# A transformer block on one core: token numbers and gate passes in front of the first transposes, inner sums behind accumulator sums, weight sums loaded in front of x

## The chip, the cores and the metric

The kernel runs on one core of a Trainium2 chip. The core has engines with instruction queues of their own: TensorE (PE; its weight loads are shown apart, as PEld), VectorE (DVE), ScalarE (ACT), GpSimd (POOL) and SyncE (SP), and 16 DMA engines that all queues share. Each engine works its queue in order. The metric is the device time of one execution in microseconds.

## The reference

`x` holds 32 sequences of 128 tokens with 512 features. Each sequence has a condition row `t` of 512 numbers, and a mask over its tokens, which is true for the last few (the padding) only.

```
emb = silu(t) @ ada_w + ada_b                  # shift, scale, gate: 3 x 512
norm = where(mask, layernorm(x)*(1+scale) + shift, 0)
ssm  = gelu(norm @ ssm_w1 + ssm_b1) @ ssm_w2 + ssm_b2
     + gelu(norm @ bwd_w1 + bwd_b1) @ bwd_w2 + bwd_b2
x    = x + gate * where(mask, ssm, 0)
ff   = silu(t) @ ffada_w + ffada_b             # shift, scale, gate again
n    = layernorm(x)*(1+scale_ff) + shift_ff
out  = x + gate_ff * (gelu_tanh(n @ ff_w1 + ff_b1) @ ff_w2 + ff_b2)
```

All is float32. The weights ssm and bwd are 512 x 512 each, ff_w1 is 512 x 1024 and ff_w2 is 1024 x 512. The two flips in the reference cancel, since the inner functions work on single tokens.

## The kernel before

**First block, masked tokens only.** The masked tokens are numbered through all sequences into "slots". There are 512 slots in four tiles of 128 (a run-time loop at the end takes what is over). `find_slots(h)` finds for half h (256 slots) the token number of each slot: two small matmuls of `pick` against `rank` into a PSUM bank, then a comparison, a sum and an addition on VectorE (lines 221 to 238). `gather_slots` fetches these tokens' rows of x with two indirect DMAs that POOL issues (line 241). `modulation_matmuls` (line 260) multiplies silu(t) with columns of ada_w: parts 0 and 1 (shift, scale) as `pm_ss`, part 2 (gate) as `pm_g` in four passes, one for each 128 of the 512 features. `slot_part` (line 288) spreads modulation rows over slots with a matmul. A tile is normalised and modulated (`modulated`, line 166), transposed on TensorE and copied by ACT (`transposed_slots`, line 175), goes through `hidden` (line 182, matmul L188, Gelu on ACT) and `project` (line 196, L203), and `finish_slots` (line 296, L209, L210 and L298) adds gate and x and stores the result to `x1_rows` in DRAM. Weights w1, w2, fw1, ada_f, fw2 and x are loaded by SP in the order of the code. The tile `ada_f` takes the place of `ada_a`, so its load waits for the last gate pass.

**Second block, all tokens.** It works on four pairs p of 8 sequences (1024 tokens). A pair has two sides of four sequences. `take_first_half` (line 670) overwrites the masked rows of the loaded x by rows of `x1_rows`, with one indirect DMA of POOL for each sequence. Both products use Strassen-Winograd's seven products of 2 x 2 blocks, the first one twice: its seven outer products are called streams (1, 2, 5, 6, 3, 7, 4, in that order), and each is made of seven inner products P1 to P7. `TokenBlocks.one(j)` (line 768, L775) makes the outer sums of the tokens' blocks. `token_sums(j, n)` (line 825) makes the inner sums, in four parts n: L835 for j = 1 (used by stream 5), L839 for 2 (stream 6), L842 for 3 (stream 7) and L845 for 4 (stream 3). The sums of the weights are made once, in the opening, and kept in DRAM as `t_rows`; `load_weights(j)` (line 847, L852) loads one of them into a tile that it shares with the gates of the second product.

Each stream has two PSUM banks, e and a. `phase` (line 897, matmul L906) does one inner product and what follows it: P5's bank is copied by ACT (L920); `seed` copies or adds a to e after P1 (L952 on ACT, L950 on VectorE); P6's result is added to a kept sum into e (L931); P7 and P4 give sums on VectorE (L936, L941). `with_p5` (L957) and `after` (L986, L990) are sums on POOL that L931 reads. The Gelu is ACT's (L868). `window` (line 995) runs two streams against each other: in position n = 0 to 6 new P5, new P1, old P3, old P7, new P2, new P6, old P4, and after each position whatever `put(w, n, ...)` filled in. Window w has new stream STREAMS[w] and old stream STREAMS[w-1]. Streams 1 and 2 of the first pair are written out by hand (lines 1206 to 1232). Those of the next pair are started during the second product (`SecondProduct`, line 1014, matmul L1093), whose steps are filled in the same way (lines 1311 to 1358); there SP also stores the output (L1073) and loads the x of the pair after next (L328).

All five engines take their instructions in the order of the code, which nothing rearranges. PSUM tiles come from pools of two or three banks for each tag (`ps_t` "tr", `ps_h` "h", `ps_o` "o"), and a new tile waits for the one that held its bank before.

Of the kernel before, what the change touches and what calls it, by code (L numbers as in the profile page):

```python
# [9 lines left out]
F32 = mybir.dt.float32  # L10
# [12 lines left out]
def kernel(  # L23
# [51 lines left out]
    P = 128  # L75
# [144 lines left out]

    def tokens_of(picked, slots, n, name, pool):

        pl = ps_t.tile([P, 512], F32, tag="tr", name=f"pl_{name}")
        for c in range(n):
# [24 lines left out]

    def find_slots(h):  # L250
        part = slice(h * NC // 2, (h + 1) * NC // 2)
        return tokens_of(pick[:, ts(h, NH)], slot_col[:, part], NC // 2, f"s{h}", ssm)

    def gather_slots(token_i):
        both = xp.tile([P, 2, D], F32, tag="x", name=f"xc_{len(xc)}")
        for c in range(NC // 2):
            gather(both[:, c], token_i[:, c : c + 1])
            xc.append(both[:, c])
# [16 lines left out]
    def modulation(pm, mod, ada, modb, lo, hi):  # L275

        modulation_matmuls(pm, ada, lo, hi, range(KC))
        modulation_rows(pm, mod, modb, lo, hi)
# [9 lines left out]
    def slot_part(at, j, pool, tag):  # L288
        return of_slots(pick, at, mod1, j, pool, tag, f"part{j}_s{at}")
# [201 lines left out]
    pm = ps_o.tile([P, 512], F32, tag="o", name="pm_ss")  # L491
    modulation(pm, mod1, ada_a, modb_a, 0, 2)
    rows = [(slot_part(c, 1, ps_o, "o"), slot_part(c, 0, ps_h, "h")) for c in range(2)]
    pm = ps_o.tile([P, 512], F32, tag="o", name="pm_g")
    xT_s = ssm.tile([P, KC, NH], F32, tag="xT", name="xT_s0", bufs=2)
    xT_t = ssm.tile([P, KC, NH], F32, tag="xT", name="xT_s1", bufs=2)
    xn = group_of_tiles("s")
    mv, rstd = statistics(xc, "s01")
    xn_s = [
# [4 lines left out]
    ]  # L504
    modulation_matmuls(pm, ada_a, 2, 3, range(2))
    fw1 = fwp.tile([P, KC, FF], F32, name="fw1")
# [13 lines left out]
    transposed_slots(xn_s[0], xT_s[:, :, ts(0, P)], "s0")  # L520
    modulation_matmuls(pm, ada_a, 2, 3, range(2, 3))
    token_i = find_slots(1)
    gather_slots(token_i)
    transposed_slots(xn_s[1], xT_s[:, :, ts(1, P)], "s1")
    modulation_matmuls(pm, ada_a, 2, 3, range(3, KC))
    ptr = ps_t.tile([P, 512], F32, tag="tr", name="ptr_b")
# [122 lines left out]
    sp = straight.enter_context(tc.tile_pool(name="sp", bufs=1, side="right"))  # L649
    gs = [keep_gate(c, slot_part(c, 2, ps_o, "o")) for c in (2, 3)]  # L650
    modT = const.tile([P, KC, 3 * B], F32, name="modT")
# [560 lines left out]
    now.do(2, "P1")  # L1212
    now.do(1, "P2", "P5", "P6")
    of_x[0].one(4)
# [9 lines left out]
    now.with_p5(2, "12")  # L1224
    now.token_sums(1, 2)
    now.token_sums(1, 3)
    now.do(2, "P2", "P6")
    for n in range(2):
        now.token_sums(2, n)
# [3 lines left out]
    for p in range(NP):  # L1233
# [7 lines left out]
        if p:  # L1241
            for n, at in enumerate(((1, 3), (1, 4), (1, 6))):
                put(*at, now.token_sums, 2, 1 + n)
        for n, at in enumerate(((1, 6), (2, 1), (2, 1), (2, 3)) if p else ((2, 1), (2, 1), (2, 3), (2, 3))):
            put(*at, now.token_sums, 3, n)
        for n, at in enumerate(((2, 4), (2, 4), (2, 6), (2, 6))):
            put(*at, now.token_sums, 4, n)
# [71 lines left out]
        if more_pairs:  # L1319
# [29 lines left out]
            if p + 2 < NP:  # L1349
                x_of[p + 2] = [[], []]  # L1350
                put(11, lambda: x_of[p + 2][0].extend(load_side(p + 2, 0)))
                put(13, lambda: x_of[p + 2][1].extend(load_side(p + 2, 1)))
            put(12, lambda: nxt["p"].do(1, "P2", "P6"))
            put(13, lambda: nxt["p"].load_weights(2))
        for step in range(2, len(ORDER)):
            second.step(step)
            for f in fill.get(step, ()):
                f()
# [120 lines left out]
```

## Time and profile before

| | us |
|---|---|
| Median of 3 runs | 465.48 (463.76 to 468.08) |
| The profiled execution's own time | 462.27 |
| Its span, first to last instruction | 460.6 |
| First L188 matmul (hidden layer of the slots) | 21.31 |
| First L906 matmul (streams of the first pair) | 87.81 |
| First L1093 matmul (second product of the first pair) | 131.52 |
| VectorE's L1067 in the last step of the first pair | 186.57 |

In a row of the timeline stand the start and the length in microseconds, the engine (with q: its queue, which issues a DMA), the line, the operation, the tile written and the tiles read, the shape, the number of instructions merged, and in brackets the engine's idle time before it with what ended it. In the rows of slices each digit stands for 11.5 us and gives the busy share in tenths. Weight loads run beside matmuls, so a wait is often shown at PEld.

### The profile page before, as it was taken

How to read it: one execution, taken by the hardware profiler on the slowest of the kernel's cores; microseconds unless marked ns; L12 is line 12 of the kernel's file. 1: busy time of each engine (PE TensorE's matmuls, PEld its weight loads, DVE VectorE, ACT ScalarE, POOL GpSimd, SP SyncE). 2: the span in 40 equal slices, each digit the busy share in tenths (PEclk: the TensorE clock that was granted, in tenths of full speed). 3: DMA queues.
4: the chain of work that ended last, by engine and by line, in shares of the span. 5: the costliest groups of instructions: out<-in, count | busy, mean ns of one | idle time of the engine just before them, and what ended most of it. 6: DMA issues, size and time to landing. Idle time of an engine off the chain costs nothing.

```text
span 460.6 us, 5827 instructions
## 1 busy us (share of the span) xinstructions
PE 447.5 (97%) x2000; PEld 364.8 (79%) x2000; DVE 331.0 (72%) x538; ACT 175.4 (38%) x380; POOL 157.5 (34%) x153
## 2 busy tenths in 40 slices
PE   6899999989999999999999999999999999999995
PEld 2385385677888888888888888888888888888884
DVE  4649768999779739986787498867973995434645
ACT  3122021744355371344454614444446154552000
POOL 6210083038981000489700005887000026560000
PEclk9999999999999999999999999999999999999999
DMA  8999835693306743823077248220872342222022
GB/s 273 386 406 360 322 130 85 204 310 94 141 5 216 103 94 110 324 93 139 1 228 112 73 162 311 91 97 3 236 107 70 133 165 80 81 88 97 0 84 102
DMA packets 82419, 70.42 MB, mean 153 GB/s; under 512 B 63168, under 2 KB 63696, under 8 KB 81362
## 3 DMA queue, kind: packets, MB, share of 16 engines
q1 hardware_dynamic: 67298, 57.03, 39.6%
q0 software_dynamic: 4480, 11.66, 7.0%
q10 hardware_dynamic: 10608, 1.32, 2.0%
q8 instruction: 17, 0.28, 0.2%
q14 instruction: 16, 0.13, 0.1%
HBM read 56.83 MB, written 13.17 MB: 152 GB/s over the span
## 4 chain that ended last, share of the span: by engine, by line
PE 74%; DVE 10%; SPq 4%; DMA 3%; issue 3%; ACT 3%; POOL 2%; ACTq 0%; DVEq 0%; POOLq 0%
PE a_o L1093 17%; PE a_m L906 16%; PE e_o L1093 13%; PE e_m L906 12%; PE ph_s L188 6%; PE po_s L203 4%; SPq L745 4%; DMA tw<-t_rows 2%; ACT xT L728 1%; DVE sx L835 1%; DVE xT L726 1%; DVE s L775 1%; PE part_s L283 1%; PE pm_f L263 1%; PE last L1093 1%
## 5 line engine op out<-in xcount | busy, mean ns | idle before, releaser
L957 POOL TENSOR_TENSOR ha<-p_m,ha 128x512 f32<-128x512 f32 x20 | 26.0, 1298 | 151.3 <-ACT ha L964 142.0
L1093 PE MATMUL e_o<-fw,ha 128*128 128x256 f32 x256 | 57.9, 379 | 0.0
L728 ACT ACTIVATE xT<-xT,modT 128x128 f32<-128x128 f32 x112 | 44.1, 480 | 30.8 <-DMA xT<-xn 30.8
L1093 PE MATMUL a_o<-t,hb 128*128 128x256 f32 x240 | 54.1, 379 | 0.0
L1093 PEld LDWEIGHTS e_o<-fw,ha 128*128 128x128 f32 x256 | 48.7, 190 | 6.6
L1093 PEld LDWEIGHTS a_o<-t,hb 128*128 128x128 f32 x240 | 45.6, 190 | 6.2
L674 POOL DMA_INDIRECT x<-x_rows,slot_i x32 | 36.0, 1126 | 29.3 <-DMA x_rows<-t_s 18.0
L868 ACT ACTIVATE hb<-hb,biasT 128x256 f32<-128x256 f32 x64 | 29.0, 500 | 29.1 <-POOL hb L990 19.4
L957 POOL TENSOR_TENSOR hb<-p_m,hb 128x512 f32<-128x512 f32 x20 | 29.1, 1454 | 19.2 <-DVE hb L936 18.9
L920 ACT COPY p_m<-e_m 128x512 f32<-128x512 f32 x27 | 15.8, 585 | 49.1 <-PE e_m L906 49.1
L964 ACT COPY ha<-e_m 128x512 f32<-128x512 f32 x32 | 18.5, 578 | 27.5 <-PE e_m L906 25.9
L1093 PE MATMUL e_o<-fw,s 128*128 128x256 f32 x128 | 28.9, 379 | 0.0
L1093 PE MATMUL a_o<-fw,ha 128*128 128x256 f32 x128 | 28.9, 379 | 0.0
L1093 PE MATMUL a_o<-t,s 128*128 128x256 f32 x128 | 28.9, 379 | 0.0
L188 PE MATMUL ph_s<-xT_s,w 128*128 128x256 f32 x128 | 28.6, 382 | 0.0
L203 PE MATMUL po_s<-w,h_s 128*128 128x512 f32 x64 | 28.6, 592 | 0.0
L188 PEld LDWEIGHTS ph_s<-xT_s,w 128*128 128x128 f32 x128 | 24.0, 190 | 4.6 <-ACT h_s L192 1.5
L1093 PEld LDWEIGHTS e_o<-fw,s 128*128 128x128 f32 x128 | 24.3, 190 | 3.3
L1093 PEld LDWEIGHTS a_o<-t,s 128*128 128x128 f32 x128 | 24.3, 190 | 3.3
L1093 PEld LDWEIGHTS a_o<-fw,ha 128*128 128x128 f32 x128 | 24.3, 190 | 3.3
L868 ACT ACTIVATE ha<-e_m,biasT 128x256 f32<-128x256 f32 x48 | 20.0, 468 | 15.4 <-PE e_m L906 14.0
L931 DVE TENSOR_TENSOR e_m<-a_m,ha 128x512 f32<-128x512 f32 x20 | 13.9, 697 | 16.4 <-POOL ha L957 6.6
(210 smaller groups left out, 869.2 us busy)
## 6 DMA issues: line engine op xcount, KB each, us to landing
tw<-t_rows SPq DMA_DIRECT2D x16, 896.0 KB, 5.1
x<-in_x_dram SPq DMA_DIRECT2D x16, 512.0 KB, 6.6
gate<-gate_rows POOLq DMA_DIRECT2D x8, 1024.0 KB, 5.1
out_dram<-x SPq DMA_DIRECT2D x15, 512.0 KB, 3.0
xT<-xn SPq DMA_DIRECT2D x92, 64.0 KB, 2.5
fw<-in_L_cond_ff_w_dram SPq DMA_DIRECT2D x2, 2048.0 KB, 10.6
ada_f<-in_L_cond_ffada_w_dram SPq DMA_DIRECT2D x4, 768.0 KB, 15.9
ada_a<-in_L_cond_ada_w_dram SPq DMA_DIRECT2D x4, 512.0 KB, 5.4
```

The lines of the kernel that those rows point to most:

```text
L188: nc.tensor.matmul(ph[:, :n], w[:, k, ts(f, P)], xT[:, k, :], start=(k == 0), stop=(k == KC - 1))
L203: nc.tensor.matmul(po, h[f][:, ts(i, P)], w[:, f, :], start=(f == 0), stop=(f == HC - 1))
L674: nc.gpsimd.indirect_dma_start(out=xs[i // G][i % G // 2][:, i % 2], out_offset=None, in_=x1_rows[:slots, :], in_offset=bass.IndirectOffse ...
L728: nc.scalar.activation(out, src, AF.Identity, bias=shift, scale=scale)
L745: queues[b % len(queues)].dma_start(dst[ts(q, R), b], src[ts(b, R), q])
L868: nc.scalar.activation(dst[:, n], src[:, n], AF.Gelu_apprx_tanh, bias=biasT[:, f : f + 1])
L906: nc.tensor.matmul(bank[:, ts(n, QT)], self.w_block(j, product)[:, ts(n, P)], self.x_block(j, product), start=(product in ("P1", "P5") and ...
L920: nc.scalar.copy(p5, e)
L931: nc.vector.tensor_tensor(e, a, p5, add)
L957: nc.gpsimd.tensor_tensor(self.place(RESULT[j], c), self.p5[j], other, ALU.add)
L964: nc.scalar.copy(self.place(RESULT[j], c), src)
L1093: nc.tensor.matmul(part, src[:, k, ts(i, P)], w[product][:, k, :], start=(last and k == 0), stop=True, skip_group_check=True,)
```

## The change

It has five parts.

1. `tokens_of` and `find_slots` take the PSUM bank as an argument. The second half's `find_slots` and `gather_slots` move up, directly behind `pm_ss`, and use a bank of `ps_h`. All four gate passes of `pm_g` are done in one place, in front of the first transposes; before, two were there, one stood behind each of the two transposes.
2. The gate of slot tile 3 is spread into a bank of `ps_h` in place of `ps_o`.
3. In the hand-written start of the first pair, stream 1's P5 comes before its P2, and `token_sums(1, 2)` and `(1, 3)` come behind stream 2's P2 and P6, so that on VectorE L931 stands in front of them.
4. In the windows, `token_sums(3, n)` and `(4, n)` move to later positions in the first pair; in the later pairs one part, `token_sums(3, 2)`, moves from (2, 1) to (2, 3), behind the L936 there.
5. In steps 11 to 13 of the second product, `load_weights(2)` of the next pair is issued in front of the load of side 1 of the x of the pair after next.

```diff
-    def tokens_of(picked, slots, n, name, pool):
+    def tokens_of(picked, slots, n, name, pool, bank=(ps_t, "tr")):
-        pl = ps_t.tile([P, 512], F32, tag="tr", name=f"pl_{name}")
+        pl = bank[0].tile([P, 512], F32, tag=bank[1], name=f"pl_{name}")
...
-    def find_slots(h):
+    def find_slots(h, *bank):
...
     modulation(pm, mod1, ada_a, modb_a, 0, 2)
+    gather_slots(find_slots(1, (ps_h, "h")))
...
-    mv, rstd = statistics(xc, "s01")
+    mv, rstd = statistics(xc[:2], "s01")
...
-    modulation_matmuls(pm, ada_a, 2, 3, range(2))
+    modulation_matmuls(pm, ada_a, 2, 3, range(KC))
...
     transposed_slots(xn_s[0], xT_s[:, :, ts(0, P)], "s0")
-    modulation_matmuls(pm, ada_a, 2, 3, range(2, 3))
-    token_i = find_slots(1)
-    gather_slots(token_i)
     transposed_slots(xn_s[1], xT_s[:, :, ts(1, P)], "s1")
-    modulation_matmuls(pm, ada_a, 2, 3, range(3, KC))
...
-    gs = [keep_gate(c, slot_part(c, 2, ps_o, "o")) for c in (2, 3)]
+    gs = [
+        keep_gate(2, slot_part(2, 2, ps_o, "o")),
+        keep_gate(3, slot_part(3, 2, ps_h, "h")),
+    ]
...
     now.do(2, "P1")
-    now.do(1, "P2", "P5", "P6")
+    now.do(1, "P5", "P2", "P6")
...
     now.with_p5(2, "12")
-    now.token_sums(1, 2)
-    now.token_sums(1, 3)
     now.do(2, "P2", "P6")
+    for n in range(2, 4):
+        now.token_sums(1, n)
...
-        for n, at in enumerate(((1, 6), (2, 1), (2, 1), (2, 3)) if p else ((2, 1), (2, 1), (2, 3), (2, 3))):
+        for n, at in enumerate(((1, 6), (2, 1), (2, 3), (2, 3)) if p else ((2, 3), (2, 3), (2, 4), (2, 4))):
             put(*at, now.token_sums, 3, n)
-        for n, at in enumerate(((2, 4), (2, 4), (2, 6), (2, 6))):
+        for n, at in enumerate(((2, 4), (2, 4), (2, 6), (2, 6)) if p else ((2, 6), (2, 6), (3, 1), (3, 1))):
             put(*at, now.token_sums, 4, n)
...
                 put(11, lambda: x_of[p + 2][0].extend(load_side(p + 2, 0)))
-                put(13, lambda: x_of[p + 2][1].extend(load_side(p + 2, 1)))
             put(12, lambda: nxt["p"].do(1, "P2", "P6"))
             put(13, lambda: nxt["p"].load_weights(2))
+            if p + 2 < NP:
+                put(13, lambda: x_of[p + 2][1].extend(load_side(p + 2, 1)))
```

## The prediction

> **What bounds the kernel now.** I read the page's busy times first, then its slices, then the timeline of each stretch in which TensorE pauses, then the waits and the landing times of the transfers.
>
> ```profile
> PE 447.5 (97%) x2000; PEld 364.8 (79%) x2000; DVE 331.0 (72%) x538; ACT 175.4 (38%) x380; POOL 157.5 (34%) x153
> DVE  4649768999779739986787498867973995434645
> DMA  8999835693306743823077248220872342222022
> ```
>
> TensorE is busy for 447.5 of 460.6 us, so no reordering can win more than 13 us, and most of that lies in the first 6 us and in the starts of short matmuls. The digits (11.5 us each) show two other things: the DMA engines are full in the first five slices (0 to 55 us), and VectorE is full in slice 8 (92 to 104 us). The pauses of TensorE lie in these places, with what stands in front of them:
>
> ```profile
> 33.04 1.23 DVE L317 TENSOR_TENSOR t<-fw 128x1024 f32<-128x1024 f32 x1 [2.15 <-DMA fw<-in_L_cond_ff_w_dram]
> ...
> 52.11 0.42 DVE L639 TENSOR_SCALAR modb_f<-modb_f 32x512 f32<-32x512 f32 x1
> ...
> 52.60 0.69 DVE L209 TENSOR_TENSOR t_s<-po_s,b 128x512 f32<-128x512 f32 x1
> ...
> 60.62 1.77 POOL L674 DMA_INDIRECT x<-x_rows,slot_i  x1 [0.31 <-issue]
> ...
> 64.17 0.69 DVE L706 BATCH_NORM_STATS2 st<-x 128x6 f32<-128x512 f32 x1 [1.05 <-DMA x<-x_rows,slot_i]
> ...
> 89.80 0.73 PEld L906 LDWEIGHTS e_m<-xT,fw 128*128 128x128 f32 x4 [0.50 <-ACT e_m L952]
> ...
> 96.36 1.74 POOL L957 TENSOR_TENSOR hb<-p_m,hb 128x512 f32<-128x512 f32 x1 [18.91 <-DVE hb L936]
> 96.89 3.44 DVE L835 TENSOR_TENSOR sx<-xT 128x512 f32<-128x512 f32 x2
> 98.07 1.71 POOL L957 TENSOR_TENSOR ha<-p_m,ha 128x512 f32<-128x512 f32 x1
> 100.58 0.68 DVE L931 TENSOR_TENSOR e_m<-a_m,ha 128x512 f32<-128x512 f32 x1
> 101.32 0.73 PEld L906 LDWEIGHTS e_m<-s,fw 128*128 128x128 f32 x4 [1.65 <-DVE e_m L931]
> ...
> 103.23 1.17 POOL L674 DMA_INDIRECT x<-x_rows,slot_i  x1 [3.45 <-DMA x<-in_x_dram]
> ...
> 120.02 0.70 DVE L931 TENSOR_TENSOR e_m<-a_m,ha 128x512 f32<-128x512 f32 x1 [2.03 <-POOL ha L986]
> ```
>
> From 33.04 (ff_w1 landed) VectorE runs without a break of more than 0.15 us to 52.53, and L209, the first step towards the second x1 store, starts 0.08 after that. At 101.32 TensorE has waited for L931, which sat on VectorE behind the inner sums of L835.
>
> ```profile
> 189.86 1.59 SPq L328 DMA_DIRECT2D x<-in_x_dram  x2
> 191.50 0.46 SPq L852 DMA_DIRECT2D tw<-t_rows  x1
> 198.68 1.10 PE L906 MATMUL e_m<-xn_sy,tw 128*128 128x256 f32 x4 [0.52 <-DMA tw<-t_rows]
> ```
>
> The weight sums of stream 6 are issued behind two x loads, land at 198.55, and TensorE has waited for them.
>
> I count a pause as the time between two matmul starts above their usual 0.216 us, and add about 0.1 for the slower first matmul after it: 0.36 at 89.80, 0.25 at 93.51, 0.26 at 94.63, 1.51 at 101.32, 0.48 at 105.26, 0.40 at 110.14, 0.27 each at 120.78 and 122.78, 0.76 at 198.68, 0.3 at 289.62.
>
> **The change, part by part.**
>
> *Opening.* Two gate passes move from behind the first transposes to in front of them (1.04 us each, at 17.90 and 20.10), the token numbers of the second half (matmuls 0.71; VectorE 0.42 + 0.42 + 0.16; two POOL gathers 1.06 + 0.98) from 18.9 to about 11.5. On TensorE the token matmuls fall into the 0.79 wait for the modulation rows. The four gate passes run 14.2 to 18.1, where it had waited 1.25 for xn_s. Second transposes then end at about 19.5 instead of 20.18, the ACT copy (0.58) follows, and L188 starts at 20.3 to 20.9 instead of 21.31: I take 0.8 early. On VectorE the 1.0 us fits before the first gather lands (13.73). On POOL the gathers stand before rstd (15.75): ready at 13.3, they end at about 15.7, so rstd slips by 0.1 to 0.5; its cover is TensorE's gate passes. ada_f, which waits on SP for the last gate pass, is issued 3 us earlier, into a full queue.
>
> TensorE's 0.8 is not the end's. The chain from 33.04 to the second x1 store is VectorE's, and only the 0.08 before L209 is TensorE's. Of the rest, modT and the weight sums (L657, L581) come 0.7 earlier and so may leave the third gather alone, which took 1.77 beside them against 1.00 for its neighbours: 0 to 0.7 saved on the way to 64.17 and so to the transposes at 79.06, where TensorE waits for xn (L718, ends 79.40). The second gathers' 512 KB now pass in front of w1 and w2: at 387 GB/s (1 MB took 2.71 us) 1.36 us later, against ssm_w1's landing at 17.16 and use at 20.3, bwd_w1's at 19.87 and use after 26. Behind w2 they no longer delay ff_w1, but it lands after the same bytes; I bound that at 0.5 either way. Sum: -0.35, between -0.9 and +0.5.
>
> The first gathers landed 4.7 us after their issue, beside ada_w, and moved 333 GB/s of one 1.5 us stretch against 63 for SP's queue. The Trainium skill (DMA: Bandwidth & Descriptors, Queues, rings and completion order) says that each DMA engine takes turns between queues packet by packet. By this rule the gathers take about half of the engines, and w1 is 1.36 us late at most, by the row all of that at once; neither brings ssm_w1 past 18.5, so the sum is the same by both.
>
> *P5 before P2 (line 1213).* The copy L952 stands behind 16 scalings on ACT until 89.17; now P5 (0.86) runs beside it. P6 still starts after the second block sum (90.76), L931 waits for P6 instead of p_m and starts at 92.35, not 92.75: -0.4 for everything on VectorE up to L1182. The 0.36 is gained once; 93.51 and 94.63 move with it.
>
> *Inner sums behind accumulator sums (0 to 131 us).* L931 of stream 2 is put ahead of two L835, but it also reads ha, which POOL's second L957 writes. Shifted by 0.4, that ends between 97.67 + 1.27 (POOL's time alone at 111.34) and 97.67 + 1.71 (beside VectorE): 98.94 to 99.38; I take the upper, since one L835 still runs beside it. L931 ends at 99.7 to 100.1, the two L835 add 1.0, and L839 starts at 100.6 to 101.1 against 101.19: VectorE wins 0.1 to 0.55. (What now waits behind L931, two L835 and then L839, is first read by TensorE in stream 5's P3, at 108.0, and stream 6's P5, at 106.2.) From there to the sum of stream 5's P7 (L936, 110.81) it has the same instructions and is full; the pauses at 101.32, 105.26 and 110.14 change places rather than add up. TensorE's own slack there (111.51 against 111.97) lets it gain 0.6 to 1.0 by 112. Next late is POOL: six gathers and six sums without a break from 103.23 to L931 at 120.02, released by the x load, whose issue stands behind L1182. Issued 0.4 earlier into DMA engines that were 73% busy at 96 to 98, it lands 0 to 0.45 earlier. So -0.3, between -0.85 and 0; the 120.78 pause stays. Rows of later pairs (one L842 behind L936) show no pause: 0.
>
> The two L835 took 1.75 beside POOL and 0.68 alone. The Trainium skill (SBUF — State Buffer, Who interferes with whom) says that a VectorE instruction with two SBUF inputs and a reading GpSimd instruction exclude each other, the later one waiting whole. This agrees, and speaks against the change: the time in which L835 was locked out is now spent waiting for L957. By the rule the second L957 ends at 99.38 and VectorE wins 0.1; by the row of POOL alone 0.55. POOL's chain allows the same either way.
>
> *Weight sums in front of x (line 1351).* SP waits at 189.86 for an output store; tw's tile is free when L1067 ends (187.26), so it can go after the store's issue at 188.40, 3.1 us earlier. It took 5.9 to 7.0 us with x beside it: lands 194.3 to 195.5, needed at 198.0. -0.76, and -0.3 at 289.62; nothing in the last two pairs, which load no x. Behind it on SP stand only these x loads, and the next issue is at 204.99; x lands up to 2.3 later (896 KB): 195.5 for the tile of the gather at 198.48.
>
> *Banks.* pl_s1 and one gate tile move to the other pool, whose third-last tile is free by 35.5: 0.
>
> **Sum:** -0.35 - 0.3 - 0.76 - 0.3 = -1.7. The profiled execution took 462.27 (span 460.6): 460.6 after. The median shown, 465.48, is 3.2 above it; shifted alike, 463.8.
>
> **Rivals.**
> - *All pauses pay in full.* 0.8 + 3.26 (89 to 110) + 1.06 = 5.1: 460.4. For it: TensorE is 97% busy, and each pause stands on it. Against: VectorE full at 98 to 112, L718 at 79.4.
> - *It does nothing that lasts:* POOL and DMA keep their times and the tw landing is replaced by another wait: 465.3. For it: the full DMA queue and POOL's chain.
> - *Slower: x behind tw.* POOL's gathers are in order, with L957 behind them. If tw takes 7.04 from 188.4 and x 4.9 after it (191.45 to 196.32), x lands at 200.4, 2 us late for 198.48. POOL's slack to L931 (204.65, less the 0.76) is 1.7 after a landing at 197.6, so it decides from 199.3 on; 1.1 lost in each of two pairs, less the 1.7 of the sum: +0.5, 466.0, and a microsecond more for each half microsecond that x lands later still. Against: the three transfers together ended at 198.55.
>
> **Chances:** forecast 0.62, all pauses 0.10, nothing 0.17, slower 0.11. About 1% (4.7 us) is what a measurement of this kernel tells from no change. Only the first rival with a little spread passes it on one side (0.08), and a heavier version of the last on the other (0.05). The forecast's own range is 462.4 to 465.3; with the rivals, and medians of three that came from 463.76 to 468.08, 461.0 to 466.4.
>
> **What would show it.** L188 starts near 20.5, yet L209 of the second store stays near 52.5; L931 near 99.5 behind POOL; TensorE's pause at 120.8 remains; none before 6's P5 near 197. Wrong if ff_w1 lands more than 1 us off 33.04, if POOL's gathers start late in pairs 1 and 2, or if TensorE keeps the 0.8 at 79.

## The result, and the profile after

The changed kernel takes 465.05 us (median, 462.11 to 466.86) against 465.2 (462.04 to 469.57) of the kernel before, measured side by side: a ratio of 0.9992, with a 95% interval of 0.9974 to 1.0010. There is no difference that can be told. The profiled executions differ by more: 462.27 us before (span 460.6), which is close to the fastest it showed, and 465.32 after (span 463.6), which is close to its median. So their difference of 3.05 us is not the effect of the change. What it contains has to be taken apart stretch by stretch.

The page of the changed kernel, in the rows that were shown of before (busy times, and the slices of VectorE and of the DMA engines, which are now 11.6 us each):

```profile
PE 448.9 (97%) x2000; PEld 364.4 (79%) x2000; DVE 330.6 (71%) x538; ACT 175.7 (38%) x380; POOL 159.8 (34%) x153
DVE  4649778998669739996787498957963985433645
DMA  8999836693206653923077259321872432213022
```

The work is the same (TensorE 1.4 us busier, and POOL 2.3). The slices look the same too, so a gain or a loss of a microsecond doesn't show on the page. The timeline shows it. Its rows for the places that the prediction named, in the changed kernel:

```profile
32.82 1.22 DVE L317 TENSOR_TENSOR t<-fw 128x1024 f32<-128x1024 f32 x1 [2.35 <-DMA fw<-in_L_cond_ff_w_dram]
...
52.35 0.69 DVE L209 TENSOR_TENSOR t_s<-po_s,b 128x512 f32<-128x512 f32 x1
...
91.84 0.70 DVE L931 TENSOR_TENSOR e_m<-a_m_alone,p_m 128x512 f32<-128x512 f32 x1 [0.49 <-ACT ha L964]
...
95.46 1.73 POOL L957 TENSOR_TENSOR hb<-p_m,hb 128x512 f32<-128x512 f32 x1 [18.57 <-DVE sx L835]
95.98 1.76 DVE L835 TENSOR_TENSOR sx<-xT 128x512 f32<-128x512 f32 x1
97.16 1.71 POOL L957 TENSOR_TENSOR ha<-p_m,ha 128x512 f32<-128x512 f32 x1
98.90 0.70 DVE L931 TENSOR_TENSOR e_m<-a_m,ha 128x512 f32<-128x512 f32 x1 [1.16 <-POOL ha L957]
99.65 1.13 PE L906 MATMUL e_m<-s,fw 128*128 128x256 f32 x4 [0.48 <-DVE e_m L931]
```

ff_w1's first reader (L317) starts 0.22 earlier, L209 starts 0.25 earlier, and the third gather (60.22) still takes 1.76. L931 of stream 2 starts at 98.90 where it started at 100.58. It now waits for POOL's second L957, as was foretold, and TensorE goes on at 99.65 instead of 101.32. Up to here the change has won 1.67 us. Then the same trace loses all of that and more:

```profile
103.08 1.12 POOL L674 DMA_INDIRECT x<-x_rows,slot_i  x1 [4.21 <-DMA x<-in_x_dram]
...
104.50 1.77 POOL L674 DMA_INDIRECT x<-x_rows,slot_i  x1 [0.30 <-issue]
...
106.58 2.09 POOL L674 DMA_INDIRECT x<-x_rows,slot_i  x1 [0.31 <-issue]
...
112.85 1.27 POOL L957 TENSOR_TENSOR ha<-p_m,ha 128x512 f32<-128x512 f32 x1
...
114.15 0.70 DVE L931 TENSOR_TENSOR e_m<-a_m,ha 128x512 f32<-128x512 f32 x1 [1.79 <-POOL ha L957]
...
114.91 1.13 PE L906 MATMUL e_m<-xn_sy,tw 128*128 128x256 f32 x4 [1.26 <-DVE e_m L931]
```

The first of the six gathers begins 0.15 earlier than before, but the second and third take 1.77 and 2.09 us where they took 0.99 and 1.01. All six together take 8.22 us instead of 6.56. The L957 behind them starts at 112.85 (before: 111.34), and VectorE's L931 and then TensorE wait for it. By 122.3 TensorE is 1.49 us *behind* its place in the trace of before. The weight sums, on the other hand, do what they should:

```profile
189.98 0.41 SPq L852 DMA_DIRECT2D tw<-t_rows  x1
...
190.86 2.34 SPq L328 DMA_DIRECT2D x<-in_x_dram  x2
...
199.48 1.03 PE L906 MATMUL e_m<-xn_sy,tw 128*128 128x256 f32 x4
```

The wait for tw in front of this matmul is gone. TensorE's place moves by -0.76 here and by -0.30 at 290. But the second and the third pair each lose a little again, in a pause at 215 and one at 306. These are the rows of the second pair in the changed kernel, and then two rows of the kernel before:

```profile
197.16 0.69 DVE L936 TENSOR_TENSOR hb<-a_m,hb 128x512 f32<-128x512 f32 x1 [0.68 <-PE a_m L906]
...
202.72 1.28 POOL L957 TENSOR_TENSOR ha<-p_m,ha 128x512 f32<-128x512 f32 x1
...
212.47 0.70 DVE L931 TENSOR_TENSOR e_m<-a_m,ha 128x512 f32<-128x512 f32 x1 [1.78 <-POOL ha L986]
...
214.49 0.68 DVE L950 TENSOR_TENSOR e_m<-a_m,ha 128x512 f32<-128x512 f32 x1
...
215.22 0.73 PEld L906 LDWEIGHTS e_m<-xT,tw 128*128 128x128 f32 x4 [0.41 <-DVE e_m L950]
```

```profile
200.92 1.29 POOL L957 TENSOR_TENSOR ha<-p_m,ha 128x512 f32<-128x512 f32 x1
...
213.25 0.68 DVE L950 TENSOR_TENSOR e_m<-a_m,ha 128x512 f32<-128x512 f32 x1
```

The part of `token_sums(3, ·)` that moved to (2, 3) stands behind L936, which waits 0.68 us for TensorE. POOL's L957 starts 1.80 us later than before and L950 1.24 later, while TensorE at 210 is 0.73 behind; it then waits for L950 and loses 0.27. The largest such loss is in the last pair, first in the changed kernel, then VectorE's two rows of the kernel before:

```profile
379.63 0.69 DVE L936 TENSOR_TENSOR hb<-a_m,hb 128x512 f32<-128x512 f32 x1 [1.24 <-PE a_m L906]
...
383.74 1.65 POOL L957 TENSOR_TENSOR ha<-p_m,ha 128x512 f32<-128x512 f32 x1 [8.04 <-ACT p_m L920]
...
384.17 1.50 DVE L845 TENSOR_TENSOR s<-s,xn_sy 128x256 f32<-128x256 f32 x1
...
385.60 0.69 DVE L950 TENSOR_TENSOR e_m<-a_m,ha 128x512 f32<-128x512 f32 x1
...
386.34 1.13 PE L906 MATMUL e_m<-xn_sy,tw 128*128 128x256 f32 x4 [0.77 <-DVE e_m L950]
```

```profile
381.97 0.42 DVE L845 TENSOR_TENSOR s<-s,xn_sy 128x256 f32<-128x256 f32 x1
382.35 0.70 DVE L950 TENSOR_TENSOR e_m<-a_m,ha 128x512 f32<-128x512 f32 x1
```

The part of `token_sums(3, ·)` that moved to (2, 3) now stands behind L936, which waits 1.24 us for TensorE, so one L842 (0.6) more stands between L936 and L950. That is enough for the last L845 to meet POOL's L957: it takes 1.50 instead of 0.42, L950 is late, and TensorE loses 1.03 us.

The whole account of the two traces, by TensorE's place at these times: -0.54 by the first L906 matmul, -0.37 from there to 97 (P5 first), -0.27 to 112 (the order of the sums), +2.67 to 130, -0.76 between 195 and 210 (tw), +0.30 to 280 (of it 0.27 in the pause at 215), -0.29 to 300 (tw), +0.31 to 365 (of it 0.27 at 306), +0.56 at 372 and +1.03 at 384 (both behind L950), and +0.40 near 400, where TensorE waits for the last weight sums. The sum is +3.04. The step at 372 is no effect of the change: it lies between 0 and 0.62 in the other traces, with and without the edit of the later pairs.

### The profile page after: what moved, and what is told of

Same layout as the page of the kernel before. It is cut to its first block, busy times and chain, and to the rows that moved or that the text cites. A ratio compares the mean times of both kernels' runs of the same rounds, so it can differ in the third digit from the quotient of the medians.

```text
span 463.6 us, 5827 instructions
## 1 busy us (share of the span) xinstructions
PE 448.9 (97%) x2000; PEld 364.4 (79%) x2000; DVE 330.6 (71%) x538; ACT 175.7 (38%) x380; POOL 159.8 (34%) x153
## 4 chain that ended last, share of the span: by engine, by line
PE 72%; DVE 8%; DMA 5%; SPq 4%; POOL 4%; issue 3%; ACT 3%; POOLq 0%; ACTq 0%; DVEq 0%
PE a_o L1093 17%; PE a_m L906 14%; PE e_o L1093 13%; PE e_m L906 11%; PE ph_s L188 6%; PE po_s L203 6%; SPq L745 4%; DMA x<-in_x_dram 2%; POOL x L674 1%; DMA xc<-in_x_dram,token_i_s 1%; DMA tw<-t_rows 1%; ACT xT L728 1%; PE part_s L283 1%; POOL ha L957 1%; PE pm_f L263 1%
## 5 line engine op out<-in xcount | busy, mean ns | idle before, releaser
L957 POOL TENSOR_TENSOR ha<-p_m,ha 128x512 f32<-128x512 f32 x20 | 26.2, 1311 | 151.9 <-ACT ha L964 142.0
L674 POOL DMA_INDIRECT x<-x_rows,slot_i x32 | 38.1, 1192 | 30.1 <-DMA x_rows<-t_s 18.0
L957 POOL TENSOR_TENSOR hb<-p_m,hb 128x512 f32<-128x512 f32 x20 | 29.3, 1464 | 18.9 <-DVE sx L835 18.6
L931 DVE TENSOR_TENSOR e_m<-a_m,ha 128x512 f32<-128x512 f32 x20 | 14.0, 698 | 21.6 <-POOL ha L957 9.5
L188 PE MATMUL ph_s<-xT_s,w 128*128 128x256 f32 x128 | 28.6, 381 | 0.5 <-issue 0.5
L188 PEld LDWEIGHTS ph_s<-xT_s,w 128*128 128x128 f32 x128 | 24.0, 190 | 5.2 <-ACT h_s L192 1.5
```

Source lines behind the costliest of these rows:

```text
L188: nc.tensor.matmul(ph[:, :n], w[:, k, ts(f, P)], xT[:, k, :], start=(k == 0), stop=(k == KC - 1))
L674: nc.gpsimd.indirect_dma_start(out=xs[i // G][i % G // 2][:, i % 2], out_offset=None, in_=x1_rows[:slots, :], in_offset=bass.IndirectOffse ...
L931: nc.vector.tensor_tensor(e, a, p5, add)
L957: nc.gpsimd.tensor_tensor(self.place(RESULT[j], c), self.p5[j], other, ALU.add)
```

## Experiments

For each kernel the traces are compared matmul by matmul: "TensorE's place" is the start of a matmul minus the start of the same matmul in the profile of before. Each comparison ran beside the kernel before on the same chip. The ratio with its 95% interval is the one on record; it differs from the quotient of the two medians by up to 0.001. The parts are called opening (1 and 2 of the change), P5 first and inner sums (3), window sums (4) and weight sums (5).

**e1: the changed kernel without the window sums.**

```diff
-        for n, at in enumerate(((1, 6), (2, 1), (2, 3), (2, 3)) if p else ((2, 3), (2, 3), (2, 4), (2, 4))):
+        for n, at in enumerate(((1, 6), (2, 1), (2, 1), (2, 3)) if p else ((2, 1), (2, 1), (2, 3), (2, 3))):
...
-        for n, at in enumerate(((2, 4), (2, 4), (2, 6), (2, 6)) if p else ((2, 6), (2, 6), (3, 1), (3, 1))):
+        for n, at in enumerate(((2, 4), (2, 4), (2, 6), (2, 6))):
```

> The changed kernel with part 4 undone (window positions of token_sums 3 and 4 as before, in the first and the later pairs). Theory A, lock-out: in the changed kernel the second and third of POOL's six gathers at 103 to 113 us took 1.77 and 2.09 us because VectorE's four L842, all with two SBUF inputs, stood in one unbroken row; with one L936 and one pair of L842 alternating again they take 1.0 to 1.2, L957 starts by 111.3 instead of 112.85, and TensorE's 1.4 us pause at 114.9 is gone; the first pair's end is about 2.5 us earlier than in the changed kernel. The later pair's 0.9 us pause near 386 goes too. About 3 us faster than the changed kernel in the trace, ratio to before near 0.994. Rival B, arrival: the gathers are slow because their rows or the x tiles come late or the queue is full; then they stay at 1.7 to 2.1 whatever VectorE does, and the ratio stays near 0.999.

Measured: 463.4 us against 464.6, ratio 0.9969 (0.9941 to 0.9998). In its trace the pauses at 114.9, 117.4 and 386 are gone. But the pause that the inner sums removed at 101 is back 4 us later: TensorE is at -1.57 at 101 and at -0.63 by 105, waiting for L936. So in this trace inner sums without window sums win nothing (0.76 won, 0.94 given back).

**e2: the changed kernel with the window sums of the later pairs back; those of the first pair stay.**

```diff
-        for n, at in enumerate(((1, 6), (2, 1), (2, 3), (2, 3)) if p else ((2, 3), (2, 3), (2, 4), (2, 4))):
+        for n, at in enumerate(((1, 6), (2, 1), (2, 1), (2, 3)) if p else ((2, 3), (2, 3), (2, 4), (2, 4))):
```

> The changed kernel with only the later pairs' token_sums(3, 2) put back from (2, 3) to (2, 1). Theory C: in the later pairs L936 in front of the third L842 makes VectorE wait 1.2 us for TensorE, and in the last pair, where POOL's L957 comes early because it has no gathers, an L845 then falls beside L957 and is locked out: the 0.93 us pause at 386 goes, ratio about 0.002 below that of the changed kernel. The first pair's pauses at 114.9 and 117.4 stay. Rival D: the late start of the last pair is only a spread from execution to execution; then the pause appears or not without regard to this edit and the ratio stays near 0.999.

Measured: 462.66 against 464.6, ratio 0.9968 (0.9940 to 0.9995). The pauses at 215, 306 and 386 are gone, and the L845 in question takes 0.42 again. The surprise is the first pair: its order is that of the changed kernel, instruction for instruction, and yet the three pauses behind POOL are absent. The six gathers took 6.90 us and the first L957 started at 110.64. So it isn't the order by itself that makes these pauses, and e1 doesn't show that it is.

**e3: the kernel before with the weight sums in front of x, and nothing else.**

```diff
-                put(13, lambda: x_of[p + 2][1].extend(load_side(p + 2, 1)))
             put(12, lambda: nxt["p"].do(1, "P2", "P6"))
             put(13, lambda: nxt["p"].load_weights(2))
+            if p + 2 < NP:
+                put(13, lambda: x_of[p + 2][1].extend(load_side(p + 2, 1)))
```

> The kernel before with part 5 alone (weight sums issued in front of side 1 of x). Expected: the pauses of 0.76 at 198.7 and 0.3 at 289.6 are gone, the gathers into side 1 at 198.5 do not wait; 1.0 us less, ratio 0.998. Rival: x lands behind the gathers' time, POOL's gathers wait for x at 198 and 290, and nothing is won.

Measured: 462.31 against 464.6, ratio 0.9943 (0.9923 to 0.9963), faster than the kernel before and in a narrow band (461.3 to 463.6). In its trace both pauses on tw are gone (-0.75 and -0.29). The ratio is lower than these two explain (0.998 was expected); e12 repeats it.

**e4: the kernel before with the opening alone.**

```diff
     modulation(pm, mod1, ada_a, modb_a, 0, 2)
+    gather_slots(find_slots(1, (ps_h, "h")))
...
-    modulation_matmuls(pm, ada_a, 2, 3, range(2))
+    modulation_matmuls(pm, ada_a, 2, 3, range(KC))
...
-    modulation_matmuls(pm, ada_a, 2, 3, range(2, 3))
-    token_i = find_slots(1)
-    gather_slots(token_i)
...
-    modulation_matmuls(pm, ada_a, 2, 3, range(3, KC))
```

> The kernel before with parts 1 and 2 alone (token numbers and gate passes in front, bank of gate 3). Expected from the trace of the changed kernel, where L188 began 0.38 earlier and the first L906 0.54 earlier: 0.3 to 0.5 us less at the first L906, the pauses at 101.3, 105.3 and 110.1 as before; ratio 0.999. Rival: the 0.54 belongs to that execution (ff_w1 landed 0.2 earlier) and L906 starts at 87.8 again.

Measured: 463.93 against 464.6, ratio 0.9987 (0.9959 to 1.0016). L188 starts 0.22 earlier, and at the first L906 nothing is left (+0.09). The row below is from its trace, the start of stream 6's P5 in the third pair:

```profile
291.17 0.67 PE L906 MATMUL e_m<-xn_sy,tw 128*128 128x256 f32 x2 [1.65 <-DMA tw<-t_rows]
```

Here tw, still behind the x loads, cost 1.60 us more than in the profile of before. So the 0.3 that the prediction read off that one profile is not what this wait always costs.

**e5 to e7: the weight sums together with one other part each.** The bands of e1 and e2 (4.3 and 5.1 us) were wider than that of e3 (2.3 us), and the question was which part brings the spread. e5 has the edits of e4 and e3 together. e6 has that of e3 and the one below (P5 first and inner sums), and e7 that of e3 and only the first two lines of it.

```diff
-    now.do(1, "P2", "P5", "P6")
+    now.do(1, "P5", "P2", "P6")
...
-    now.token_sums(1, 2)
-    now.token_sums(1, 3)
     now.do(2, "P2", "P6")
+    for n in range(2, 4):
+        now.token_sums(1, n)
```

> The kernel before with the opening (the second half's token numbers and all gate passes in front of the first transposes) and with the weight sums in front of x; the first pair keeps its old order. With the weight sums alone eleven executions lay between 461.3 and 463.6 (median 462.3). Theory S (what spoils the rest is the new order of the first product, parts P5 before P2 and the sums behind): this one keeps the narrow band, median 461.8 to 462.4, none above 464; L188 0.2 to 0.4 earlier and nothing of it left at 79. Rival O (the opening itself brings late transfers, since the second gathers now run beside ada_a and w1): median near 463.4, some executions above 464.5.

> The kernel before with P5 before P2, with the inner sums of stream 1 behind the accumulator sums of stream 2, and with the weight sums in front of x; the opening and the sums inside the windows stay as before. Theory S: the median rises to 463 to 463.6 and some executions pass 464.5, though the pause at 101.3 shrinks from 1.4 to 0.65 us and the profile can be as low as 460. Rival O: it keeps the narrow band of the weight sums alone and gains the 0.4 to 0.9 us that the order wins at 101: median 461.4 to 462.0. In both, if TensorE is 0.9 ahead at 101 and 0.3 or less by 115, POOL's chain of gathers and sums has taken the gain.

> The kernel before with P5 before P2 alone and the weight sums in front of x; the inner sums stay where they were. It separates the two edits of the first order. Expected by the terms of the prediction: the pause at 89.8 goes, L931 of stream 1 comes 0.4 earlier, and the wait at 101.3 for L931 behind L835 stays at 1.4 us or more, so no more than 0.4 us lasts to 101: median 461.9 to 462.4, narrow. Rival: P5's earlier place moves the x1 store and with it the x load and the gathers, and so brings the spread: median above 462.8.

Measured, each against 463.87: e5 462.85, ratio 0.9976 (0.9948 to 1.0004); e6 462.86, ratio 0.9988 (0.9965 to 1.0011); e7 463.36, ratio 0.9981 (0.9953 to 1.0009). All three have the wide band (4.0 to 6.4 us), so neither theory named the right part. e7's median is the one that its rival gave, but e12 shows the wide band without P5 first too. The traces are of more use. In every kernel that has P5 first, TensorE's place moves by -0.36 or -0.37 between 85 and 97 (e1, e2, e6 to e11 and the changed kernel), though e5, which has not, shows -0.26 there, and e4 -0.03. In e6 the inner sums again win 0.76 at 101 and give 0.96 back at 105.

**e8: the changed kernel with the weight sums back behind x.**

```diff
+                put(13, lambda: x_of[p + 2][1].extend(load_side(p + 2, 1)))
             put(12, lambda: nxt["p"].do(1, "P2", "P6"))
             put(13, lambda: nxt["p"].load_weights(2))
-            if p + 2 < NP:
-                put(13, lambda: x_of[p + 2][1].extend(load_side(p + 2, 1)))
```

> The changed kernel with the weight sums back behind the x loads. Theory W (in most executions the weight sums land later than in the profile of before, so that this part is worth 2 us or more in the median, as before against the weight sums alone shows: 464.6 against 462.3): median 466.8 to 467.8, 2 us above the changed kernel's. Rival (the part is worth what the two pauses of the profile are, 0.68 and 0.29): median 465.8 to 466.2.

Measured: 464.0 against 463.87, ratio 1.0003 (0.9975 to 1.0031). Both numbers were missed. In its trace the pause on tw is back at 198.4, with 1.22 us, and at 289 there is none. So the part is worth 1.2 us in this trace (a step of +0.53 there, against -0.68 in the changed kernel), but not the 2 us of theory W. The medians don't show 1.2: the changed kernel wasn't measured in this series, and the expected medians were taken from another. The trace has the changed order of the first pair and none of its pauses, with the first L957 at 110.22; and it has the pause at 306 (+0.27) and that in the last pair (+1.04 at 384). At 215 it has none, after it lost time to tw.

**e9: one gather fewer in front of POOL's sums.** If POOL's chain of gathers and sums sets the first pair, then L957 should come forward with the gathers out of its way.

```diff
-            put(2, 6, take_first_half, p + 1, x_next, range(G, G + 2))
-            put(3, 4, take_first_half, p + 1, x_next, range(G + 2, G + 3))
+            put(2, 6, take_first_half, p + 1, x_next, range(G, G + 1 + (p > 0)))
+            put(3, 4, take_first_half, p + 1, x_next, range(G + 1 + (p > 0), G + 2 + (p > 0)))
+            if p == 0:
+                put(4, 4, take_first_half, p + 1, x_next, range(G + 2, G + 3))
```

> The changed kernel with one row gather fewer in front of POOL's first sums of the first pair: the sixth gather goes behind L986, the seventh behind the next four sums; instructions and data are the same. Theory P (POOL's chain of gathers and sums decides the first pair; L931 and TensorE stand behind it where the first L957 begins later than about 111.5, as at 112.85 in the profile of the changed kernel, and not where it begins at 110.2 or 110.6): the first L957 begins 1.3 earlier, at 109 to 111.5 whatever the x load does; no pause of over 1 us at 115; by 130 TensorE is 0.2 to 1.2 us ahead of before; median 0.3 to 1.2 under the changed kernel's in the same call. Rival (the stretch is an accident of one execution and seldom sets the end): same median within 0.3. In both the pause of 0.9 at 385 in the last pair stays.

Measured: 465.14 against 464.96, ratio 0.9999 (0.9970 to 1.0027), and the same as the changed kernel beside it (465.06). L957 did come forward, to 108.85, but the profiled execution (468.73, the slowest of its series) lost 5.85 us between 97 and 130 instead of winning. VectorE and then POOL in this trace:

```profile
108.49 0.69 DVE L950 TENSOR_TENSOR e_m<-a_m,ha 128x512 f32<-128x512 f32 x1
109.09 4.04 DVE L845 TENSOR_TENSOR xT<-xT,xn_sy 128x512 f32<-128x512 f32 x1
113.05 0.41 DVE L845 TENSOR_TENSOR s<-s,xn_sy 128x256 f32<-128x256 f32 x1
```

```profile
108.85 1.28 POOL L957 TENSOR_TENSOR ha<-p_m,ha 128x512 f32<-128x512 f32 x1
110.08 1.27 POOL L957 TENSOR_TENSOR hb<-p_m,hb 128x512 f32<-128x512 f32 x1
111.30 1.26 POOL L986 TENSOR_TENSOR ha<-ha 128x512 f32<-128x512 f32 x1
```

L957 now starts while VectorE has two L845 to go. The L845 at 109.09, 0.69 us elsewhere, takes 4.04: it ends 0.57 after POOL's third sum. POOL's three sums follow each other without a gap, and VectorE's instruction stays out for all three. Everything queued behind it, L936 with TensorE behind it, waits. The Trainium skill (SBUF — State Buffer, Who interferes with whom) says that between a VectorE instruction with two SBUF inputs and a reading GpSimd instruction the one issued first keeps the shared ports for its whole length and the other blocks fully. The trace agrees that VectorE is kept out, and shows that it can last for more than one instruction: the wait was 3.35 us (4.04 less the usual 0.69), not 1.3. A row of POOL's sums doesn't always do this. In the same trace two L957 follow each other without a gap at 96.22 and 97.92, and VectorE's L835 at 96.74 got in between them (1.76); every other trace has it so at this place. What decides is not shown. What follows for the theory is that the gathers in front of L957 hold POOL back until VectorE is through with its L845. With the gathers moved, the wait moved to VectorE, in this one trace at least; the medians show neither gain nor loss.

**e10: the changed kernel once more.**

> The changed kernel itself once more, for the same chip as the others and for a second profile. Theory P: the pauses at 114.9, 117.4 and 122.3 come back only if the first L957 behind the gathers begins after 111.5; otherwise they are absent and TensorE is about 1.0 ahead of before by 130. Both: the pause of 0.93 at about 385 is there again, and the wait for the last weight sums near 400 of 0.3 to 0.6 as well. Rival (the order itself causes the three pauses): they are there with the first L957 at 110 to 111 too.

Measured: 465.06 against 464.96, ratio 1.0006 (0.9980 to 1.0032), the first result again. In this profile L957 starts at 111.49. Two small pauses (0.49 at 116.0 and 0.50 at 120.9) stand behind it, and the one of 1.4 at 115 isn't there. TensorE loses 1.02 from 112 to 130 and is 0.13 late there, so the limit of 111.5 in the expectation is not the right one (the table below has a better one). The pauses at 215 and 306 (0.27 each) are there, and the last pair's is (+1.03 at 384).

**e11: the edits of e2 and e9 together** (the later pairs' sums back, and fewer gathers in front of POOL's sums).

> The changed kernel with the sums of stream 3 in the later pairs back in their old place, and with the sixth and seventh gather of the first pair behind POOL's sums. By the terms that the profiles so far show (opening 0.2 to 0.4, P5 first 0.37, first windows' sums 0.25, weight sums 0.69 and 0.29, no pause at 385): about 1.8 to 2.1 under before where the x load is late or not, so a median of 0.9 to 1.3 under the changed kernel in this call, at or under the weight sums alone. Rival (only the weight sums count, the rest is spread): same as the weight sums alone or up to 1 above.

Measured: 463.09 against 464.96, ratio 0.9975 (0.9939 to 1.0012), from 460.61 to 467.4, the widest band of the twelve experiments. It is not shown to be better than the weight sums alone. It differs from e9 by the later pairs' sums alone, and its median is 2.05 lower in the same series, though the bands overlap. In its profile x landed 5.4 us after its issue, so that L957 began at 111.86, behind VectorE's L845, and the long wait of e9 didn't occur. TensorE lost 2.30 from 112 to 130 all the same, in four pauses, the longest of 0.84 at 128.5 behind L931. The pauses at 215, 306 and 386 are absent.

**e12: the weight sums alone, once more.**

> The kernel before with the weight sums in front of x alone, once more: its eleven executions lay in a band of 2.3 us with a ratio of 0.9943, while each kernel that has this part and something more spread over 4 to 6 us with ratios of 0.997 to 0.999. Theory L (that band was luck; the part is worth its two pauses, 0.7 and 0.3): ratio 0.996 to 0.9985 here, some executions above 464. Rival (the other parts bring the spread): ratio 0.9925 to 0.996 again, none above 464.

Measured: 463.64 against 464.96, ratio 0.9968 (0.9941 to 0.9996), up to 466.46. So the narrow band of e3 was luck, and the part is worth about 0.3 to 0.6%. Of the two parts that were measured alone (this one and the opening) it is the one that is measurably faster than the kernel before, and it is so twice. Beside it the changed kernel took 465.06. Its profile answers the question that e2 opened, POOL first and then TensorE:

```profile
106.35 2.43 POOL L674 DMA_INDIRECT x<-x_rows,slot_i  x1 [0.31 <-issue]
109.09 1.83 POOL L674 DMA_INDIRECT x<-x_rows,slot_i  x1 [0.30 <-issue]
...
113.55 1.27 POOL L957 TENSOR_TENSOR ha<-p_m,ha 128x512 f32<-128x512 f32 x1
```

```profile
115.61 1.13 PE L906 MATMUL e_m<-xn_sy,tw 128*128 128x256 f32 x4 [0.32 <-DVE e_m L931]
...
118.05 0.70 PE L906 MATMUL e_m<-xT,fw 128*128 128x256 f32 x2 [0.44 <-DVE e_m L950]
```

This kernel has the *old* order of the first pair, and it shows the three pauses (0.48, 0.61, 0.49) in the same places. They belong to a late L957 and not to the new order alone.

**The first pair in all traces.** The table takes the twelve profiles in which the six gathers stand in front of L957 (all but e9 and e11). Columns: issue and landing of the first x tile, the time of the six gathers together, the start of the first L957, the same minus 111.34 (its start in before), and TensorE's place at 130.

| kernel | x issued | x landed | gathers | L957 | L957 - 111.34 | TensorE at 130 |
|---|---|---|---|---|---|---|
| before | 97.38 | 102.38 | 6.56 | 111.34 | 0 | 0 |
| changed | 96.47 | 102.22 | 8.22 | 112.85 | +1.51 | +1.49 |
| e10 (changed) | 96.75 | 101.58 | 7.50 | 111.49 | +0.15 | +0.13 |
| e8 (same first pair) | 96.78 | 100.99 | 6.82 | 110.22 | -1.12 | -1.11 |
| e2 (same first pair) | 97.20 | 101.35 | 6.90 | 110.64 | -0.70 | -0.68 |
| e1 | 96.56 | 101.54 | 6.77 | 110.71 | -0.63 | -0.62 |
| e6 | 97.07 | 102.00 | 6.84 | 111.24 | -0.10 | -0.10 |
| e7 | 98.71 | 102.89 | 7.46 | 112.73 | +1.39 | +1.41 |
| e5 | 96.71 | 100.82 | 7.45 | 110.68 | -0.66 | -0.66 |
| e4 | 97.44 | 101.31 | 7.69 | 111.40 | +0.06 | +0.05 |
| e3 | 97.31 | 101.18 | 7.70 | 111.28 | -0.06 | -0.04 |
| e12 (same kernel as e3) | 97.94 | 102.21 | 8.94 | 113.55 | +2.21 | +2.19 |

The last two columns agree within 0.02 us in every row. In seven rows TensorE had that place already at 112. There POOL keeps step with VectorE, and with it with TensorE: VectorE's L706, the first instruction behind L950, starts 0.01 to 0.02 before the fifth gather ends, and L957 starts 1.33 to 1.35 after L706. The rows show it for before and then for e3, where the first gather had started 1.20 earlier:

```profile
108.62 1.39 POOL L674 DMA_INDIRECT x<-x_rows,slot_i  x1 [0.31 <-issue]
110.00 0.68 DVE L706 BATCH_NORM_STATS2 st<-x 128x6 f32<-128x512 f32 x1
111.34 1.28 POOL L957 TENSOR_TENSOR ha<-p_m,ha 128x512 f32<-128x512 f32 x1
```

```profile
108.46 1.49 POOL L674 DMA_INDIRECT x<-x_rows,slot_i  x1 [0.30 <-issue]
109.93 0.69 DVE L706 BATCH_NORM_STATS2 st<-x 128x6 f32<-128x512 f32 x1
111.28 1.28 POOL L957 TENSOR_TENSOR ha<-p_m,ha 128x512 f32<-128x512 f32 x1
```

In e8 and e2, which have the changed order, L957 also keeps a fixed distance, 0.64 and 0.65. In these nine rows what TensorE had won or lost up to 112 lasts (in e8 and e2 it even gains 0.25 and 0.24 more). In the other three L957 comes later than that: 3.60 after L706 in the changed kernel, 1.94 in e10, 2.98 in e12. There TensorE waits and loses 2.67, 1.02 and 1.62. So POOL's chain decides only where its gathers fall behind VectorE's row. From the first L906 matmul to 130, the four profiles with the changed order moved by -0.88 (e2), -0.89 (e8), +0.39 (e10) and +2.03 (changed): the new order does win time, in two of four executions. What decides which it will be isn't shown. It isn't the landing of x alone: in e12 x landed 0.17 earlier than in before, and L957 came 2.21 later.

**The later pairs in all traces.** The pauses at 215 and 306 (0.26 to 0.27 each) and the one of 1.03 at 384 are in all four traces that have the edit of the later pairs (the changed kernel, e8, e9, e10; e8 lacks the one at 215) and in none of the other ten. The medians sort in the same way: the four kernels' ratios are 0.9992, 1.0003, 0.9999 and 1.0006, those of the nine experiments without this edit 0.9943 to 0.9988. Most of the intervals overlap, but no ratio is out of order. So this edit costs about 1.6 us by the traces, and e2, which takes back nothing else, is the experiment that shows it.

## Why the prediction was right, and where it wasn't

The forecast was no difference that can be told, with 463.8 us, and the result is 465.05, ratio 0.9992. That there is no difference came true, but not for the forecast's reason: its -1.7 us lies outside the measured interval (-1.2 to +0.5), and the result is nearest to the rival "It does nothing that lasts" (465.3). The range was wide enough for both. Inside the forecast, the terms went like this.

- **Opening (-0.35):** right in size. In the changed kernel the first L906 stands at -0.54. Over the nine traces that have the opening, the median there is -0.23, over the other five +0.07. But "I take 0.8 early" for L188 was too much: -0.38 here, and -0.22 to -0.44 in seven of the nine (+0.36 and +0.19 in e2 and e9). The step that failed is the cover of rstd. The two gathers in front of it started at 14.09 and not at 13.3. Its slip was put at 0.1 to 0.5 and was 0.73 (15.75 to 16.48), and TensorE's gate passes, which ended at 18.4, didn't hide it:

```profile
14.78 3.62 PE L263 MATMUL pm_g<-ada_a,sT 128*32 128x512 f32 x8
18.33 0.66 PE L179 MATMUL ptr_s<-ident,xn_s 128*128 128x128 f32 x4
19.55 0.66 PE L179 MATMUL ptr_s<-ident,xn_s 128*128 128x128 f32 x4 [0.56 <-DVE xn_s L172]
```

  The second transposes wait 0.56 for xn_s; before, they followed without a wait. The third gather at 60 us was freed in five of the nine traces with the opening (1.16 in e1 and e5, 1.17 in e2, 1.00 in e4 and e8) and not in the other four (1.76 here, 1.77 in e9) nor in the five without it (1.76 to 1.77). That is the "0 to 0.7" of the prediction. At the first L906 it made no difference: the median of the five is -0.22, that of the four -0.25.
- **P5 before P2:** right. -0.4 was said, -0.37 is shown. The 0.36 pause is gone (e5 shows that part of it can go without the edit), and L931 starts at 91.84, which is 92.75 less 0.54 and less 0.37.
- **Inner sums:** right for what happens up to 112 (L931 ends at 99.60, POOL's L957 holds it, TensorE was to gain 0.6 to 1.0 by 112 and gains 0.64 there, -0.54 to -1.18). Right too that POOL's chain of gathers and sums is next. Wrong is the size of that chain. It was taken as fixed, with only the x load's landing to move it "0 to 0.45 earlier" (and as six gathers; a seventh, 1.01 at 115.23, stands between its sums). x landed 0.15 earlier, in that range, though issued 0.91 earlier. But the six gathers took 8.22 instead of 6.56, a term that the sum didn't have. "Between -0.85 and 0" became +2.03 and +0.39 in the two profiles of this kernel, and -0.88 and -0.89 with the same first pair in e2 and e8, all counted from the first L906.
- **Later pairs ("show no pause: 0"):** wrong in all three later pairs, and this is the largest lasting miss: +0.27, +0.27 and +1.03, together about +1.6, which alone is almost the whole -1.7. The edit was read as one L842 behind L936, and that L936 waits for TensorE (0.68 in the second pair, 1.24 in the last) wasn't counted. In the second and third pair VectorE, the gathers and POOL's L957 behind them slip (L957 starts at 202.72 where it started at 200.92), and TensorE in the end waits for L950. The last pair has no gathers: L957 comes at once and meets the L845 that stands one L842 later.
- **Weight sums (-0.76 and -0.3):** right in these traces, -0.76 and -0.30 (-0.75 to -0.76 and -0.29 to -0.30 in every trace that has the part). Other traces with tw behind x show that the wait it removes varies: 1.8 us at 291 in e4 and 1.2 at 198 in e8, where e8 has none at 289.
- **The slower rival, x behind tw,** needed x to land after 199.3 in the second pair. It landed at 198.79 in the changed kernel, 198.80 in e2 and 198.96 in e3, so the point was nearly reached but not passed. The load before that one was put at 195.5 ("up to 2.3 later") and landed at 197.24, 4.1 later than before; the gathers between 195 and 203 followed each other without a longer break, so nothing waited for it.
- **The median "shifted alike":** a weak place. The profile of before was one of its fastest executions (462.27 of a median of 465.2), and that a sum made against it carries to the median was not shown. Taken over all the traces, the parts are -0.3 (opening), -0.9 to +2.0 (first pair from the first L906 on, with a mean of +0.2 over four), -0.76 and -0.30 (tw) and +1.6 (later pairs), together about +0.4, with -0.7 at the best. What was measured is -0.15 in the medians, and by the ratio's interval -1.2 to +0.5. So the gains are there, and the later pairs' edit and the late gathers cancel them.

What stays open: how the remaining spread of some 4 us, which all kernels have, divides between the opening's loads, the first pair, and the last weight sums (near 400 TensorE lost 0.4 to 0.9 us more than in before in six of the fourteen traces, and at most 0.1 more in the others). And whether the gathers are held up by VectorE was not tried apart from it; the next section gives what speaks for it.

## What to carry to other kernels

Before a pause of TensorE is counted as a gain, look for the engine whose chain ends last some 20 us later, and ask whether the edit moves *that* chain's start: here 1.1 us won between 88 and 101 lasted to 0.9 in two of four profiles, and was lost in the two in which POOL's first sum came late behind its six gathers. An edit that is read as harmless in a loop has to be followed through every pair, and above all through the one that lacks the work beside it, the last: here one sum moved behind an instruction that waits for TensorE cost 0.27, 0.27 and 1.03 us. And where one profile is near the fastest of a wide band, its waits should be looked up in a second profile before a sum is built on them.

## What the runs showed of the hardware

- **VectorE can be kept out by a row of POOL's sums, and TensorE pays twice.** In e9 VectorE's 0.69 us sum took 4.04 beside three sums of POOL (beside two at 96.74 it took 1.76). After a pause of 3.85 us beyond the usual spacing TensorE came back at half the clock. The busy times by window of e9 show it (the columns are the busy time of PE, PEld, DVE, ACT and POOL with the number of instructions, then the granted TensorE clock, the DMA share and GB/s):

```profile
105.00:110.00 5.00, 4.59 (x21) 3.49 (x21) 5.00 (x9) 2.40 (x5) 4.28 (x4) 1.00 0.15 40
110.00:115.00 5.00, 1.31 (x7) 0.83 (x5) 4.96 (x6) 0.59 (x1) 3.85 (x4) 0.92 0.02 5
115.00:120.00 5.00, 5.00 (x12) 4.03 (x13) 2.81 (x7) 1.17 (x2) 0.59 (x1) 0.50 0.39 116
```

  In the 5 us after the pause the granted clock is 0.50, and 12 matmuls are done where 22 follow in the next 5 us. Thirteen matmuls in a row stand 0.21 us further apart than before, 2.7 us in all. After the pauses of 1.4 us in the other traces only the first matmul is slower, by 0.1.
- **The time of a gather's issue goes with where it falls against VectorE's instructions.** Beside VectorE's L706, which reads one SBUF tile, they take 1.00 us (62.29 and 63.59 in the changed kernel). In the first pair they took 1.0 to 2.4, and the same VectorE instructions at the same offset gave the same time: 1.49 to 1.51 where L842 or L845, which read SBUF twice, began 0.05 before, 0.55 after and another instruction 0.88 after the gather's start (in e2, e3, e4, e5, e7, e8 and e10). With L931 and L941 at the first two of these offsets, which read PSUM and SBUF, a gather of before took 1.00 (at 107.32). So an earlier landing of x need not help: in e3 x landed 1.2 us earlier than in before, with VectorE at the same place, and the six gathers took 7.70 instead of 6.56, so that L957 started at 111.28 instead of 111.34.
- **The same load landed 3.9 to 5.8 us after its issue** (the first x tile, fourteen traces): 5.75 and 4.83 in two profiles of the changed kernel, 3.88 and 4.27 in two of the weight sums alone.
